# Attention with residual on one core: ScalarE empties the shared PSUM bank, the value bias moves to the residual, and the softmax sums take a way through DRAM

## The chip, the core and the metric

The kernel runs on one core of a Trainium2 chip. The core has five engines that each work through a queue of their own in order: TensorE (PE, matrix products, into the accumulation memory PSUM), VectorE (DVE), ScalarE (ACT), GpSimd (POOL) and SyncE (SP), which here only issues DMA transfers. The metric is device time in microseconds (us). The kernel before took 2355.27 us (median of 3 runs, 2353.17 to 2355.44).

## The reference

The input is x, 32 images of 256 channels on 32 x 32 places, in 32 bits throughout. Each image is normalised by groups of 8 channels, projected to queries, keys and values, goes through causal attention with 8 heads of 32 channels over its 1024 places, and is added to x:

```python
x = x + _L0_conv_ref(_gn(x), q_w, q_b, kv_w, kv_b)
# in _L0_conv_ref:
mask = jnp.tril(jnp.ones((S, S)), -1)                 # strictly before: place 0 sees nothing
scores = jnp.einsum('bhqd,bhkd->bhqk', q, k) / sqrt(dk)
scores = jnp.where(mask == 0, -10000.0, scores)
attn = jnp.where(mask == 0, 0.0, softmax(scores))
out = jnp.einsum('bhqk,bhkd->bhqd', attn, v)
```

For every place but the first the weights of a row add up to 1, so a bias on the values may as well be added to the result. Place 0 gets nothing, and its output is x alone.

## The kernel before

The work of one image is cut into 20 steps, written `(g, hf, k)`: g is one of two groups of four heads, hf one of two halves of 512 queries, k a block of 128 keys; half 0 has 3 steps, half 1 has 7. Steps are numbered 0 to 19 within an image below: 3 to 9 are group 0, half 1, and 13 to 19 group 1, half 1. A step's `scores` is four concurrent products of 512 queries into two pairs of PSUM banks (tile sT), an exponential of each pair on ACT (tile e), and on the diagonal a select on POOL that zeroes what a query must not see. Two steps later (LAG) `values` multiplies e with the values (tile acc), and DVE adds e onto a running sum of the group's first e tile. Behind the last step of a (g, hf), ACT copies acc to num, and one step later `sums` multiplies the running sum by ones (tile pd), so that the sums over all keys come out of PE. There are four such sums per image, in the steps 5, 12, 15 and, for the last, step 2 of the next image.

Between these, PE does the projections of the next image: eight units for queries and keys (tile pp) and four for the values (ppv), and two small products for the group averages of the image after next (pm and pv). All of pp, ppv, pm, pv and pd use one single PSUM bank (`misc`, pool ps_m with one buffer): each product must wait until the one before it has been read out. ACT reads pp, DVE reads ppv, pm, pv and pd.

The order is written by hand. `when(i, f)` puts f into step i, behind that step's scores and before its values, and `after` puts it behind the values. Each engine's queue is the order in which this loop emits its instructions:

```python
scores(*steps[i])
for f in at.get(i, ()): f()
values(*steps[i - LAG])
for f in after.get(i, ()): f()
```

An image's results are finished in the next image: DVE checks that the sums lie in a sane range, takes their reciprocals in four pieces of 128 columns, SP spreads these over 32 partitions per head (tile rb), DVE multiplies num by rb, POOL adds x and overwrites place 0, and SP writes the result.

## Time and profile before

| | |
|---|---|
| median of 3 runs | 2355.27 us |
| the profiled execution | 2354.04 us |
| its span in the trace | 2352.0 us, granted TensorE clock 0.951 |
| PE busy | 2113.2 us (90%) |
| DVE busy | 1732.8 us (74%) |
| ACT busy | 1358.9 us (58%) |
| POOL busy | 722.1 us (31%) |

The trace names an instruction by its line and tiles, "v<-ppv,v_bias" for a read of ppv and v_bias that writes v. A timeline row has the start, the duration, the engine and line, and in brackets how long the engine stood idle before it and what ended that. A row of the list of waits has the waiting engine and line, what it waited for, and then the total, the number of times and the longest. A row of the windows has for each engine its busy time, and behind POOL's the clock that TensorE was granted, 1.00 being the full one.

### The profile page before, as it was taken

The page shows a single profiled execution, that of the slowest core. Times are in us where ns is not written, and L with a number is a line of the kernel's source. Part 1 is how long each engine was busy: PE and PEld are TensorE (multiplying, and loading weights), DVE is VectorE, ACT ScalarE, POOL GpSimd, SP SyncE. Part 2 cuts the span into 40 slices and gives each one's busy share as a digit, 9 for nine tenths or more (in the row PEclk, how much of TensorE's full clock was granted, in tenths as well). Part 3 has the DMA queues.
Part 4 walks back from the last instruction along what each step waited for, and adds up shares of the span by engine and source line. Part 5 has one row for each costly group of instructions (what it writes and reads, how often), then busy time and mean ns, then how long its engine had stood idle before and what let it go on. Part 6 is the DMA issues. An engine that isn't in the chain of part 4 may idle for free.

```text
span 2352.0 us, 49835 instructions
## 1 busy us (share of the span) xinstructions
PE 2113.2 (90%) x22030; PEld 748.7 (32%) x22030; DVE 1732.8 (74%) x1641; ACT 1358.9 (58%) x1665; POOL 722.1 (31%) x689
## 2 busy tenths in 40 slices
PE   4999998899998999988999989899889999898995
PEld 1333333333333333333333333333333323333331
DVE  2577678777777777787777787777877777877787
ACT  1656655556555566555566555665555655556663
POOL 0232233322332322333223323223332233232245
PEclk9999999999999999999999999999999999999997
DMA  2001111011111010111011110111110111101001
GB/s 88 2 28 46 37 55 55 36 38 48 44 55 55 28 46 37 55 55 43 30 54 38 55 55 28 46 37 55 55 54 20 55 37 55 55 28 46 19 37 73
DMA packets 38078, 104.84 MB, mean 45 GB/s; under 512 B 4192, under 2 KB 5088, under 8 KB 37856
## 3 DMA queue, kind: packets, MB, share of 16 engines
q1 hardware_dynamic: 37856, 101.60, 11.8%
q8 instruction: 174, 2.85, 0.5%
q14 instruction: 48, 0.39, 0.1%
HBM read 34.47 MB, written 33.55 MB: 29 GB/s over the span
## 4 chain that ended last, share of the span: by engine, by line
PE 54%; DVE 40%; issue 5%; ACT 1%; DMA 0%; POOL 0%; SPq 0%; DVEq 0%; POOLq 0%; ACTq 0%
DVE e L270 24%; PE pp L130 16%; PE sT L234 12%; PE acc L265 11%; PE ppv L130 10%; PE pd L282 4%; DVE st L144 3%; DVE rec L301 2%; DVE den L290 2%; DVE rb L319 2%; DVE dev L156 1%; DVE xn L172 1%; DVE in_range L295 1%; DVE in_range L294 1%; DVE dev L157 1%
## 5 line engine op out<-in xcount | busy, mean ns | idle before, releaser
L241 ACT ACTIVATE e<-sT 128x1024 f32<-128x1024 f32 (+1 forms) x1280 | 1126.0, 939 | 629.4 <-PE sT L234 532.5
L270 DVE TENSOR_TENSOR e<-e,e 128x2048 f32<-128x2048 f32 (+3 forms) x640 | 1162.7, 1817 | 84.9 <-POOL e L247 48.7
L247 POOL TENSOR_SCALAR_AFFINE_SELECT e<-e 128x512 f32<-128x512 f32 (+1 forms) x384 | 443.3, 1162 | 1464.1 <-ACT e L241 1464.0
L234 PE MATMUL sT<-q,k 32*128 32x512 f32 (+3 forms) x6144 | 710.1, 525 | 0.5 <-ACT e L241 0.5
L265 PE MATMUL acc<-e,v 128*32 128x512 f32 (+3 forms) x6144 | 623.1, 493 | 6.7 <-POOL e L247 4.2
L130 PE MATMUL pp<-xn,wT 128*32 128x512 f32 x4096 | 494.2, 600 | 13.9 <-DVE den L288 7.8
L130 PE MATMUL ppv<-wT,xn 128*32 128x256 f32 x4096 | 297.1, 439 | 154.2 <-DVE rstd L164 143.7
L234 PEld LDWEIGHTS sT<-q,k 32*128 32x128 f32 x6144 | 299.1, 183 | 420.6 <-issue 283.2
L265 PEld LDWEIGHTS acc<-e,v 128*32 128x32 f32 x6144 | 176.4, 112 | 391.4 <-issue 309.2
L290 DVE TENSOR_TENSOR den<-den,pd 128x512 f32<-128x512 f32 x96 | 66.0, 687 | 285.0 <-PE pd L282 285.0
L320 POOL TENSOR_TENSOR rb<-rb,x 128x512 f32<-128x512 f32 x128 | 226.0, 1766 | 131.3 <-DVE rb L319 95.7
L204 DVE TENSOR_TENSOR v<-ppv,v_bias 128x512 f32<-128x512 f32 x128 | 88.0, 687 | 211.5 <-PE ppv L130 211.5
L130 PEld LDWEIGHTS ppv<-wT,xn 128*32 128x32 f32 x4096 | 132.9, 123 | 296.4 <-DVE rstd L164 146.3
L130 PEld LDWEIGHTS pp<-xn,wT 128*32 128x32 f32 x4096 | 107.0, 109 | 318.7 <-issue 201.8
L274 ACT COPY num<-acc 128x512 f32<-128x512 f32 x128 | 74.3, 580 | 224.7 <-PE acc L265 224.7
L282 PE MATMUL pd<-e,pick 128*32 128x512 f32 x1024 | 137.3, 608 | 23.4 <-DVE e L270 23.2
L189 ACT ACTIVATE q<-pp,qk_bias 128x512 f32<-128x512 f32 x128 | 88.2, 689 | 68.8 <-PE pp L130 63.6
L301 DVE RECIPROCAL rec<-den 128x128 f32<-128x128 f32 x128 | 120.2, 941 | 0.0
L189 ACT ACTIVATE k<-pp,qk_bias 128x512 f32<-128x512 f32 x128 | 88.2, 689 | 41.0 <-PE pp L130 39.3
L319 DVE TENSOR_TENSOR rb<-num,rb 128x512 f32<-128x512 f32 x128 | 91.8, 718 | 2.4 <-DMA rb<-rec 2.4
L144 DVE BATCH_NORM_STATS2 st<-x 128x6 f32<-128x512 f32 x128 | 80.1, 668 | 4.6 <-DMA x<-in_x_dram 4.6
L282 PEld LDWEIGHTS pd<-e,pick 128*32 128x32 f32 x1024 | 23.9, 108 | 125.7 <-DVE e L270 60.2
(40 smaller groups left out, 280.9 us busy)
## 6 DMA issues: line engine op xcount, KB each, us to landing
x<-in_x_dram SPq DMA_DIRECT2D x32, 1024.0 KB, 5.8
rb<-rec SPq DMA_DIRECT2D x128, 256.0 KB, 2.5
out_dram<-rb SPq DMA_DIRECT2D x64, 512.0 KB, 3.0
wn<-in_L_conv_kv_w_dram SPq DMA_DIRECT2D x2, 256.0 KB, 3.3
wn<-in_L_conv_q_w_dram SPq DMA_DIRECT2D x1, 256.0 KB, 2.8
v_bias<-in_L_conv_kv_b_dram SPq DMA_DIRECT2D x1, 128.0 KB, 3.0
qk_bias<-in_L_conv_q_b_dram SPq DMA_DIRECT2D x1, 1.0 KB, 3.3
qk_bias<-in_L_conv_kv_b_dram SPq DMA_DIRECT2D x1, 1.0 KB, 3.0
```

The lines of the kernel that those rows point to most:

```text
L130: nc.tensor.matmul(out[part], lhsT=lhsT[:, part], rhs=rhs, start=start, stop=stop, skip_group_check=True)
L144: nc.vector.bn_stats(st[:, c, :], live["x", b][:, g, c * HALF : (c + 1) * HALF])
L189: nc.scalar.activation(live[key][:, cols], pp, AF.Identity, bias=qk_bias[:, n, g : g + 1], scale=(SCALE, 1.0)[n],)
L234: nc.tensor.matmul(pairs[j // 2][:, j % 2, cols], lhsT=kk[rows, kb * P : (kb + 1) * P], rhs=q[rows, hf * HALF + of.start : hf * HALF + of. ...
L241: nc.scalar.activation(e[:, 2 * a : 2 * a + 2, c0:], pairs[a][:, :, c0:], AF.Exp)
L247: nc.gpsimd.affine_select(out=diagonal, in_=diagonal, pattern=[[0, 4], [0, n], [1, P]], compare_op=ALU.is_gt, fill=0.0, base=0, channel_mu ...
L265: nc.tensor.matmul(acc[HD * j : HD * (j + 1), of], lhsT=live["v", b][:, kb, h * HD : (h + 1) * HD], rhs=e[:, j, cols], start=k == 0, stop= ...
L270: nc.vector.tensor_add(total[:, :, of], total[:, :, of], e[:, :, cols])
L282: nc.tensor.matmul(pd[HD * j : HD * (j + 1), :], lhsT=pick[:, n, :], rhs=total[:, j, :], start=True, stop=True, skip_group_check=True,)
L301: nc.vector.reciprocal(live["rec", b][:, cols], live["den", b][:, cols])
L319: nc.vector.tensor_mul(rb[:, g, cols], num[:, g, cols], rb[:, g, cols])
L320: nc.gpsimd.tensor_add(rb[:, g, cols], rb[:, g, cols], xt[:, g, cols])
```

## The change

Four things change together.

- ACT instead of DVE reads the shared bank everywhere: the mean, the variance (with 1e-5 added as a bias), the values and the sums.
- The values carry no bias any more. DVE's last step adds the bias of the channel and x in one instruction (line 327 of the new file), and the corner copy goes to DVE too; POOL has no part in the finish.
- The sums of the four (g, hf) are each copied to SBUF by ACT and written to DRAM by SP. When all are there, `gather` reads them back as 128 rows of 64 values, DVE checks and inverts these, SP writes the inverses to DRAM, and the spread reads them from there.
- The steps to which things are given: the load two steps earlier, the pieces of the preparation to steps 4, 5, 8, 10, 16, 18 in place of 3, 5, 8, 11, 14, 16, the projections so that no two products on the shared bank stand in one step, check and inversion at step 5 of the next image, and the finish at 11, 12, 14, 15 of the next image in place of 11 to 14 behind an end that was counted one step later.

```diff
-    pick = const.tile([P, 4, HD], F32, name="pick")
...
+    pick = const.tile([P, HD], F32, name="pick")
+    nc.gpsimd.memset(pick, 1.0)
...
+        dram = tc.alloc_tile_pool(name="dram", bufs=2, space=bass.MemoryType.DRAM)
...
-            nc.vector.tensor_copy(mean, pm[:, :NG])
+            nc.scalar.copy(mean, pm[:, :NG])
...
-            nc.vector.tensor_scalar_add(rstd, pv[:, :NG], 1e-5)
+            nc.scalar.activation(rstd, pv[:, :NG], AF.Identity, bias=eps)
...
-            nc.vector.tensor_add(
-                live["v", b][:, 2 * n : 2 * n + 2, :], pp, v_bias.unsqueeze(1).broadcast_to([P, 2, C])
-            )
+            nc.scalar.copy(live["v", b][:, 2 * n : 2 * n + 2, :], pp)
...
-                    pd[HD * j : HD * (j + 1), :], lhsT=pick[:, n, :], rhs=total[:, j, :],
+                    pd[HD * j : HD * (j + 1), :], lhsT=pick, rhs=total[:, j, :],
...
+            den = small.tile([P, HALF], F32, tag="den", name=f"den_{b}_{n}")
+            nc.scalar.copy(den, pd)
             if n == 0:
-                live["den", b] = small.tile([P, HALF], F32, tag="den", name=f"den_{b}")
-                nc.vector.tensor_copy(live["den", b], pd)
-            else:
-                nc.vector.tensor_add(live["den", b], live["den", b], pd)
...
+                live["sums", b] = dram.tile([4, 4, HALF], F32, tag="sums", name=f"sums_{b}")
+            nc.sync.dma_start(out=live["sums", b][n], in_=den[::HD, :])
+
+        def spread_rows(t):
+            return t.rearrange("n j (r c) -> (n j r) c", c=ROW)
+
+        def gather(b):
+            live["rows", b] = small.tile([P, ROW], F32, tag="rows", name=f"rows_{b}")
+            nc.sync.dma_start(out=live["rows", b], in_=spread_rows(live["sums", b]))
+
+        def invert(b):
+            rows = live["rows", b]
+            nc.vector.scalar_tensor_tensor(in_range, rows, SUM_MIN, in_range, ALU.is_ge, ALU.mult)
+            nc.vector.scalar_tensor_tensor(in_range, rows, SUM_MAX, in_range, ALU.is_le, ALU.mult)
+            inv = small.tile([P, ROW], F32, tag="inv", name=f"inv_{b}")
+            nc.vector.reciprocal(inv, rows)
+            live["inv", b] = dram.tile([4, 4, HALF], F32, tag="inv", name=f"inverses_{b}")
+            nc.sync.dma_start(out=spread_rows(live["inv", b]), in_=inv)
...
-                    in_=rec[n::4, :].unsqueeze(1).broadcast_to([P // 4, 4, HALF]),
+                    in_=live["inv", b][n].unsqueeze(1).broadcast_to([4, HD, HALF]),
...
-            nc.gpsimd.tensor_add(rb[:, g, cols], rb[:, g, cols], xt[:, g, cols])
+            nc.vector.scalar_tensor_tensor(
+                rb[:, g, cols], rb[:, g, cols], v_bias_col[:, g : g + 1], xt[:, g, cols], ALU.add, ALU.add
+            )
             if hf == 0:
-                nc.gpsimd.tensor_copy(rb[:, g, 0:1], xt[:, g, 0:1])
+                nc.vector.tensor_copy(rb[:, g, 0:1], xt[:, g, 0:1])
...
-                when(b * N, lambda b=b: load(b + 2))
-                for n, f in zip((3, 5, 8, 11, 14, 16), prepare(b + 2)):
+                when(max(b * N - 2, 0), lambda b=b: load(b + 2))
+                for n, f in zip((4, 5, 8, 10, 16, 18), prepare(b + 2)):
                     when(b * N + n, f)
...
-                    when(b * N + 1 + n * N // len(units), f)
+                for n, f in zip((1, 3, 4, 6, 7, 9, 11, 13, 14, 16, 17, 19), projections(b + 1)):
+                    when(b * N + n, f)
...
-            end = (b + 1) * N + LAG + 2
-            when(end, lambda b=b: check_sums(b))
-            for c in range(BPH):
-                when(end + 1 + c, lambda b=b, c=c: invert(b, c))
-            when(end + BPH, lambda b=b: spread(b))
-            for n in range(4):
-                when(end + BPH + 3 + n, lambda b=b, n=n: finish(b, n))
+            end = (b + 1) * N + LAG + 1
+            when(end, lambda b=b: gather(b))
+            when(end + 2, lambda b=b: invert(b))
+            when(end + 2, lambda b=b: spread(b))
+            for n, at_step in enumerate((8, 9, 11, 12)):
+                when(end + at_step, lambda b=b, n=n: finish(b, n))
```

What this does to the queues is shown at two places. The first is DVE around steps 8 to 11 of image 4, before. The names carry image, group, half and key block; `dev_6` belongs to the preparation of image 6, `v_5` to the projection of image 5, `rb_3` to the finish of image 3, and the e tiles to image 4 itself.

```order
L155 TENSOR_TENSOR dev_6_2875<-mv_6_2717,mean_6_2873 128x2
L156 TENSOR_TENSOR dev_6_2875<-dev_6_2875 128x2
L157 TENSOR_TENSOR dev_6_2875<-dev_6_2875,mv_6_2717 128x2
L270 TENSOR_TENSOR e0_4_0_1_0_2708<-e0_4_0_1_0_2708,e_4_0_1_3_2788 128x2048
L204 TENSOR_TENSOR v_5_2824<-ppv_5_1_2894,v_bias_122 128x512
L270 TENSOR_TENSOR e0_4_0_1_0_2708<-e0_4_0_1_0_2708,e_4_0_1_4_2813 128x2048
L270 TENSOR_TENSOR e0_4_0_1_0_2708<-e0_4_0_1_0_2708,e_4_0_1_5_2848 128x4x384
L270 TENSOR_TENSOR e0_4_0_1_0_2708<-e0_4_0_1_0_2708,e_4_0_1_5_2848 128x4x128
L319 TENSOR_TENSOR rb_3_2863<-num_3_2185,rb_3_2863 128x512
L164 TENSOR_SCALAR rstd_6_2960<-pv_6_2955 128x2
```

The same place in the changed kernel, up to the addition that the second sum (pd) needs:

```order
L159 TENSOR_TENSOR dev_6_2915<-mv_6_2775,mean_6_2913 128x2
L160 TENSOR_TENSOR dev_6_2915<-dev_6_2915 128x2
L161 TENSOR_TENSOR dev_6_2915<-dev_6_2915,mv_6_2775 128x2
L273 TENSOR_TENSOR e0_4_0_1_0_2735<-e0_4_0_1_0_2735,e_4_0_1_3_2836 128x2048
L273 TENSOR_TENSOR e0_4_0_1_0_2735<-e0_4_0_1_0_2735,e_4_0_1_4_2860 128x2048
L273 TENSOR_TENSOR e0_4_0_1_0_2735<-e0_4_0_1_0_2735,e_4_0_1_5_2894 128x4x384
L273 TENSOR_TENSOR e0_4_0_1_0_2735<-e0_4_0_1_0_2735,e_4_0_1_5_2894 128x4x128
L326 TENSOR_TENSOR rb_3_2813<-num_3_2213,rb_3_2813 128x512
L327 SCALAR_TENSOR_TENSOR rb_3_2813<-rb_3_2813,v_bias_col_120,x_3_879 128x512
L331 COPY rb_3_2813<-x_3_879 128x1
L273 TENSOR_TENSOR e0_4_0_1_0_2735<-e0_4_0_1_0_2735,e_4_0_1_6_2924 128x4x256
```

The v addition and the read of pv have left DVE's queue, and the whole first quarter of the finish stands ahead of the last addition.

The second place is ACT in steps 8 to 11 of the same image, in the changed kernel, where these reads now stand.

```order
L244 ACTIVATE e_4_0_1_5_2894<-sT_4_0_1_5_0_2895 128x1024
L244 ACTIVATE e_4_0_1_5_2894<-sT_4_0_1_5_1_2896 128x1024
L156 COPY mean_6_2913<-pm_6_2908 128x2
L244 ACTIVATE e_4_0_1_6_2924<-sT_4_0_1_6_0_2925 128x2x256
L244 ACTIVATE e_4_0_1_6_2924<-sT_4_0_1_6_1_2926 128x2x256
L209 COPY v_5_2870<-ppv_5_1_2934 128x512
L244 ACTIVATE e0_4_1_0_0_2957<-sT_4_1_0_0_0_2958 128x1024
L244 ACTIVATE e0_4_1_0_0_2957<-sT_4_1_0_0_1_2959 128x1024
L168 ACTIVATE rstd_6_2973<-pv_6_2968,eps_75 128x2
L244 ACTIVATE e_4_1_0_1_2986<-sT_4_1_0_1_0_2987 128x1024
L244 ACTIVATE e_4_1_0_1_2986<-sT_4_1_0_1_1_2988 128x1024
L209 COPY v_5_2870<-ppv_5_2_3003 128x512
```

Each read stands behind the two exponentials of its own step. On PE, pv moves one step forward, from the step of a projection of values to a step without one, and the fourth such projection moves from step 12 to step 13.

More of the change, by code (lines that the diff above doesn't have):

```diff
@@ L26 @@
 SUM_MAX = 1.0e20
+ROW = 64
 LAG = 2
@@ L71, in tile_norm_attention_residual @@
     nc.gpsimd.memset(power, -0.5)
-    pick = const.tile([P, 4, HD], F32, name="pick")
-    nc.gpsimd.memset(pick, 0.0)
-    for n in range(4):
-        nc.gpsimd.memset(pick[:, n, n::4], 1.0)
+    pick = const.tile([P, HD], F32, name="pick")
+    nc.gpsimd.memset(pick, 1.0)
     avg = const.tile([P, P // CPG, CPG], F32, name="avg")
@@ L88, in tile_norm_attention_residual @@
     avg = avg.rearrange("p a b -> p (a b)")
-    in_range = const.tile([P, HALF], F32, name="in_range")
+    in_range = const.tile([P, ROW], F32, name="in_range")
     nc.gpsimd.memset(in_range, 1.0)
+    eps = const.tile([P, 1], F32, name="eps")
+    nc.gpsimd.memset(eps, 1e-5)
     wT = const.tile([P, NG, 3 * C], F32, name="wT")
@@ L106, in tile_norm_attention_residual @@
     nc.vector.tensor_scalar_mul(qk_bias[:, 0, :], qk_bias[:, 0, :], SCALE)
+    v_bias_col = const.tile([P, NG], F32, name="v_bias_col")
+    nc.sync.dma_start(out=v_bias_col, in_=kv_b[C : 2 * C].rearrange("(g p) -> p g", p=P))
     v_bias = const.tile([P, C], F32, name="v_bias")
@@ L118, in unshifted @@
         ps_m = tc.alloc_tile_pool(name="ps_m", bufs=1, space=PSUM)
-        pools = [xpool, work, qkpool, epool, small, ps_s, ps_o, ps_m]
+        pools = [xpool, work, qkpool, epool, small, dram, ps_s, ps_o, ps_m]
         live = {}
@@ L352, in unshifted @@
                     when(b * N + s + LAG + 1, lambda b=b, g=g, hf=hf: sums(b, g, hf), after)
-            end = (b + 1) * N + LAG + 2
-            when(end, lambda b=b: check_sums(b))
-            for c in range(BPH):
-                when(end + 1 + c, lambda b=b, c=c: invert(b, c))
-            when(end + BPH, lambda b=b: spread(b))
-            for n in range(4):
-                when(end + BPH + 3 + n, lambda b=b, n=n: finish(b, n))
+            end = (b + 1) * N + LAG + 1
[4 more added lines that the diff above has]
+                when(end + at_step, lambda b=b, n=n: finish(b, n))
         with tc.manual_schedule(engines={ENG.PE, ENG.Activation, ENG.DVE, ENG.Pool}):
```

12 lines of the change are left out of this document (removed).

## Prediction

> **What bounds the kernel now.** I read the page first, then the list of waits, then the timeline of one image, then the granted clock in small windows.
>
> ```profile
> span 2352.0 us, 49835 instructions
> PE 2113.2 (90%) x22030; PEld 748.7 (32%) x22030; DVE 1732.8 (74%) x1641; ACT 1358.9 (58%) x1665; POOL 722.1 (31%) x689
> ...
> PE ppv L130 <- DVE rstd L164: 143.7, 30, 4.9
> ...
> PE pd L282 <- DVE e L270: 23.2, 31, 2.6
> ...
> PE pp L130 <- DVE den L288: 7.8, 29, 0.3
> ```
>
> TensorE (PE) is 90% busy and every other engine has room, so PE's program order is the clock of the loop. It loses time in one place: 30 times a value projection (ppv) waits until VectorE (DVE) has read pv out of the one shared bank, 143.7 us in all, which is 29 times the 4.87 us seen below and a short one. Images 1 to 29 have it: image 0 has no image before it to finish, and 30 and 31 have none to prepare. Everything else PE waits for is small. The timeline shows why DVE is late; the rows run from step 8 of an image to its second sum, and the last one is step 8 of the next image.
>
> ```profile
> 1011.86 1.15 PE L234 MATMUL sT<-q,k 32*128 32x384 f32 x16
> ...
> 1013.04 2.92 ACT L241 ACTIVATE e<-sT 128x1024 f32<-128x1024 f32 x4 [1.86 <-PE sT L234]
> ...
> 1015.00 0.16 DVE L155 TENSOR_TENSOR dev<-mv,mean 128x2 f32<-128x2 f32 x1
> ...
> 1015.05 1.73 POOL L247 TENSOR_SCALAR_AFFINE_SELECT e<-e 128x1024 f32<-128x1024 f32 x2 [3.12 <-ACT e L241]
> ...
> 1016.72 2.28 DVE L270 TENSOR_TENSOR e<-e,e 128x2048 f32<-128x2048 f32 x1
> ...
> 1018.92 0.68 DVE L204 TENSOR_TENSOR v<-ppv,v_bias 128x512 f32<-128x512 f32 x1
> ...
> 1019.52 5.93 DVE L270 TENSOR_TENSOR e<-e,e 128x2048 f32<-128x2048 f32 x3
> ...
> 1021.05 0.24 PE L130 MATMUL pv<-dev,avg 128*32 128x2 f32 x8
> ...
> 1025.37 0.68 DVE L319 TENSOR_TENSOR rb<-num,rb 128x512 f32<-128x512 f32 x1
> 1025.97 0.14 DVE L164 TENSOR_SCALAR rstd<-pv 128x2 f32<-128x2 f32 x1
> ...
> 1026.17 3.64 PE L130 MATMUL ppv<-wT,xn 128*32 128x256 f32 x32 [4.87 <-DVE rstd L164]
> ...
> 1030.86 1.93 PE L130 MATMUL ppv<-wT,xn 128*32 128x256 f32 x32
> ...
> 1032.12 0.73 POOL L247 TENSOR_SCALAR_AFFINE_SELECT e<-e 128x512 f32<-128x512 f32 x1 [3.81 <-ACT e L241]
> ...
> 1033.60 1.07 PE L282 MATMUL pd<-e,pick 128*32 128x512 f32 x8
> ...
> 1083.54 1.15 PE L234 MATMUL sT<-q,k 32*128 32x384 f32 x16
> ```
>
> pv is finished at 1021.3, but its reader L164 stands in DVE's queue behind three sum additions and a finishing multiplication, and runs at 1025.97. The restart is dear too: the ppv at 1026.17 takes 3.64 us where the next takes 1.93, 1.71 more. The clock rows of this image and the next say why.
>
> ```profile
> 1022.50:1023.00 0.50, 0.00 (x0) 0.00 (x0) 0.50 (x1) 0.43 (x1) 0.00 (x1) 0.93 0.00 0
> 1029.50:1030.00 0.50, 0.50 (x12) 0.20 (x4) 0.12 (x1) 0.00 (x0) 0.00 (x0) 0.74 0.00 0
> 1094.18:1094.68 0.50, 0.00 (x0) 0.00 (x0) 0.50 (x1) 0.43 (x1) 0.00 (x1) 0.93 0.00 0
> 1101.18:1101.68 0.50, 0.50 (x12) 0.20 (x4) 0.12 (x1) 0.00 (x0) 0.00 (x0) 0.74 0.00 0
> ```
>
> The seventh number is the granted clock. It is half from about 1022.85 (a window's mean of 0.93) to about 1029.7 (0.74), some 6.83 us, and the same stretch returns exactly 71.68 us later, which is also the step from 1011.86 to 1083.54. 71.68 is 21 times 3.413, half of the stretch. I read this as a grid of 3.41 us on which the clock falls and recovers: PE resumes, runs at half clock up to the next line of the grid, and by this the image's period settles on whole cells, 21 of them. Without the slow restart it would be about 70.0.
>
> **The change, part by part.** *The stall at ppv goes.* ScalarE (ACT) now reads pv directly behind the two exponentials of its own step, about 3.2 us after that step's scores start, and PE wants the bank 3.3 us after. I cost this wait at 0.1 us. If ACT were a step late it would be 3 us, but ACT keeps up: its work in a step with a projection is two exponentials (1.9 us) and one copy against PE's 3.8.
>
> *What is late next* is the sum of the second group. Its matmul (pd) at step 12 needs the last addition of step 11, and DVE's new order before that is: dev chain, additions of steps 8 to 10, then the whole finish of the first quarter (multiply, add, corner copy), then that addition. The dev chain cannot start before ACT has copied the mean, and ACT does so after both exponentials of step 8; everything behind it on DVE is held as well. From the rows, with time zero at 1011.86:
>
> - dev starts at 3.14 now. The select on e at 1015.05 (3.19) shows when the exponentials are done; I add a copy of 0.2 us and take 3.35.
> - From there to the end of the three additions now takes 1025.45 − 1015.00 = 10.45, less the v addition, which leaves DVE (1019.52 − 1018.92 = 0.60): 9.85, which contains the selects of GpSimd (POOL) that share this stretch. End at 13.2.
> - Multiply 0.68, the new add 0.69, corner copy 0.1, and 0.1 for waiting on each other's output: 1.55. Then the addition of 1024 columns, 1.22. That is 16.0.
> - The select that today falls after the stall (1032.12, 0.73) now falls into this stretch: 16.7.
>
> PE could be there earlier. Its unit costs are steps between starts where nothing waits:
>
> ```profile
> 1062.19 0.61 PE L265 MATMUL acc<-e,v 128*32 128x256 f32 x8
> ...
> 1062.74 0.71 PE L234 MATMUL sT<-q,k 32*128 32x256 f32 x8
> ...
> 1063.38 1.92 PE L130 MATMUL pp<-xn,wT 128*32 128x512 f32 x16
> ...
> 1067.11 1.14 PE L234 MATMUL sT<-q,k 32*128 32x512 f32 x8
> ...
> 1080.82 1.93 PE L130 MATMUL ppv<-wT,xn 128*32 128x256 f32 x32
> ...
> 1082.57 1.04 PE L265 MATMUL acc<-e,v 128*32 128x512 f32 x8
> ```
>
> A short acc is 0.55, short scores 0.64, a projection 1.75, a full acc 0.97 (to 1083.54). With pv done at 9.4 that gives ppv, short acc, short scores, full acc: 13.3, and 0.1 for the restart, 13.4. **So PE waits 3.3 us at pd instead of 4.9 us at ppv.** The second sum starts at 16.7; today it starts at 1033.60 − 1011.86 = 21.74 with one more projection ahead of it (1.75, moved to step 13).
>
> The rest of the image, from that sum to the next step 8, takes 1083.54 − 1033.60 = 49.94. It gets the moved projection, +1.75, and loses the small waits of the list above, 0.75 at pd and 0.27 at pp: 50.7. Natural period 16.7 + 50.7 = 67.4 against about 70.0.
>
> *The clock.* A 3.3 us gap in PE is more than twice the 1.5 us (1021.3 to 1022.85) after which the clock fell here, so I expect half clock again. Bounds: no loss at all, or 1.71 as now. On the grid the next whole number of cells above 67.4 is 20, 68.27, a loss of 0.9 and inside the bounds, so I take 68.27: **3.41 us less per image.**
>
> The Trainium skill, in "TensorE: Matmul & The Clock Gate", section "What's actually happening", says that the clock is gated after at least one idle window of about 3.4 us, and that these windows run freely. The grid agrees; the fall after 1.5 us of idleness does not need a wholly idle window, and the rows decide.
>
> *Costs beside the path.*
>
> ```profile
> L274 ACT COPY num<-acc 128x512 f32<-128x512 f32 x128 | 74.3, 580 | 224.7 <-PE acc L265 224.7
> ...
> L288 DVE COPY den<-pd 128x512 f32<-128x512 f32 x32 | 20.5, 642 | 6.5 <-PE pd L282 6.5
> ...
> L294 DVE SCALAR_TENSOR_TENSOR in_range<-den,in_range 128x512 f32<-128x512 f32 x32 | 21.9, 683 | 0.0
> ...
> L301 DVE RECIPROCAL rec<-den 128x128 f32<-128x128 f32 x128 | 120.2, 941 | 0.0
> ...
> rb<-rec SPq DMA_DIRECT2D x128, 256.0 KB, 2.5
> ...
> qk_bias<-in_L_conv_kv_b_dram SPq DMA_DIRECT2D x1, 1.0 KB, 3.0
> ```
>
> ACT gains eight copies of 0.58 and two tiny reads per image, some 5 us on 42; it has 25 us of room, and PE's 3.8 us steps cover each copy. The Trainium skill, in "ScalarE: Activation LUTs", section "Rules for kernel authors", speaks against this: adds and the like belong on VectorE, up to three times faster. At three times 0.642 the eight copies would be 15 us per image, and where an exponential pair, a v copy and a num copy meet in one step (1.94 + 1.93 + 0.58 against PE's 3.4 us in step 11) PE would wait 1 us, 29 us in all. The rows contradict it for reads from PSUM in 32 bits: 580 ns on ACT, 642 on DVE.
>
> DVE loses four reciprocals (3.76), four bias additions (2.75), four den operations (2.7) and most of two checks (1.4); it gains four adds of the row L294's kind (2.75) and a reciprocal of 64 columns (0.47 by half of L301). Net about −7 us per image, but only what stands between steps 8 and 12 counts, and that is in the sum. POOL's residual adds go.
>
> The DRAM legs: den copy 0.6 after the fourth sum, then a write and a gather. Small transfers of before land in 3.0 us, so the row of sums is back 6.8 us after the fourth sum. DVE reaches its check at about 4.2 and stops there for some 2.6 us, with the statistics of the second half and two additions behind it (7.1 us of work with the check). These must be done by the mean, 17.7 + 3.35 = 21 us after the sum (step 3 starts right behind the fourth sum, in the trace at 1067.11, so 16.4 to the next step 8, plus one projection, less 0.5 of waits), so the gather may land as late as 13.9. Cover: 7 us. The inverses go out and come back in two more legs (3.0 and 2.5), near 14; the multiplication that reads them stands near 30. SP issues 13 transfers per image in place of 7, each under 0.6 us, in 68 us. All this costs nothing inside the loop.
>
> *Edges.*
>
> ```profile
> 2243.78 1.93 PE L130 MATMUL ppv<-wT,xn 128*32 128x256 f32 x32 [1.76 <-DVE v L204]
> ...
> 2303.66 1.93 PE L282 MATMUL pd<-e,pick 128*32 128x512 f32 x8 [1.96 <-DVE e L270]
> ...
> 2332.59 0.69 DVE L290 TENSOR_TENSOR den<-den,pd 128x512 f32<-128x512 f32 x1 [2.06 <-PE pd L282]
> ...
> 2338.05 2.49 SPq L309 DMA_DIRECT2D rb<-rec  x4
> ```
>
> From the last den operation to the issue of the spread it now takes 5.5 us, with nothing beside it; with a copy, three legs and a short check it will be 0.6 + 9.0 + 0.9 = 10.5, so +5, less up to 3 because POOL no longer follows with the last additions. The last two images may lose the waits of 1.76 and 1.96 in the rows, and a half clock, 0 to −5. I take zero for both together, between −5 and +5.
>
> Sum: 2354.04 (the profiled execution) − 29 × 3.41 = 2255.2; the median of the runs shown stands 1.2 above that execution, so **2256 us**.
>
> **Rivals.**
>
> 1. *The gap does not lower the clock.* The period is then the natural 67.4: 29 × 4.3 = 124 us, 2231. For it: the gap is 1.6 us shorter than now, and the page on the clock gate asks for a whole idle window, which 3.3 us is not. Against: half clock began 1.5 us into the gap. 0.12.
> 2. *DVE is not late at pd.* If selects and dev chain cost 2 us less than in today's rows, PE's wait falls under 1.5 us and the clock stays: period 13.4 + 50.7 = 64.1 up to 65.5, saving 29 × 6.2 to 7.6, 2135 to 2176. For it: POOL's residual adds no longer compete with DVE. Against: none of them stood in the stretch that I took over. 0.15.
> 3. *The gather comes late* (slower). DVE waits at its check for the row of sums in front of all additions. It decides once a leg takes over 6.6 us (13.9 = 0.6 + 2 legs); at 10 us a leg the gather lands at 20.6, the image grows by 6.7 to 74.1, 22 cells, 75.1: 29 × 3.4 more, 2454. Against: the transfers quoted above landed in 2.5 and 3.0 us. 0.06.
> 4. *The change moves the stall without gain.* If the finish on DVE holds pd 3 us longer than I sum (stt slower, more selects in between), the period falls back to 21 cells: 2355. 0.05; something between that and my forecast, 2290 to 2345: 0.10.
>
> My forecast itself, 2235 to 2290: 0.52.
>
> **Numbers.** The range 2150 to 2290 takes in the forecast, the first rival and half of the second, about 0.75 to 0.8. A difference under 0.2% (about what a measurement of this kernel can tell from none) has 0.04; slower 0.07, from the third rival and the tail of the fourth; faster 0.89.
>
> **What would show it.** Right: no wait of ppv on pv's reader; a wait of about 3 us per image of pd on DVE's additions; half clock still once per image, 68.3 us apart; ACT near 1510 us busy, DVE near 1510, POOL near 470. Wrong: pd without a wait and no half clock (second rival), DVE idle at its check for over 10 us (third), ppv waiting for ACT, or a period of 71.7.

## The result, and the profile after

The changed kernel takes 2264.35 us (median of 4 runs, 2263.33 to 2264.6) where the kernel before took 2354.82 beside it: a ratio of 0.9616, with a 95% interval of 0.9599 to 0.9633. The profiled execution took 2263.33 us, with a span of 2261.6. All lines from here on are numbered as in the file they come from; in the changed kernel L156 reads the mean, L168 pv, L209 the values and L291 the sums (all on ACT), L273 adds up e, L326 and L327 are the finish on DVE, L305 the check, L316 the spread.

The first part of the changed kernel's page:

```profile
span 2261.6 us, 50192 instructions
...
PE 2081.9 (92%) x22030; PEld 733.3 (32%) x22030; DVE 1514.2 (67%) x1417; ACT 1492.0 (66%) x1985; POOL 419.3 (19%) x494
```

The list of waits of the changed kernel:

```profile
DVE dev L159 <- ACT mean L156: 203.0, 32, 6.7
...
PE pd L286 <- DVE e L273: 92.2, 32, 3.4
...
PE ppv L134 <- ACT mean L156: 8.0, 30, 0.3
```

The wait of 143.7 us of ppv on pv's reader is gone, and PE now waits 92.2 us for DVE's additions at pd. The timeline of one image, from step 8 to the second sum (the idle time ahead of a row is in brackets):

```profile
972.15 1.15 PE L237 MATMUL sT<-q,k 32*128 32x384 f32 x16
...
975.35 1.09 DVE L159 TENSOR_TENSOR dev<-mv,mean 128x2 f32<-128x2 f32 x1 [6.74 <-ACT mean L156]
...
977.19 7.55 DVE L273 TENSOR_TENSOR e<-e,e 128x2048 f32<-128x2048 f32 x4
...
981.42 1.93 PE L134 MATMUL ppv<-wT,xn 128*32 128x256 f32 x32
...
984.53 2.26 POOL L250 TENSOR_SCALAR_AFFINE_SELECT e<-e 128x1024 f32<-128x1024 f32 x2
...
984.66 1.59 DVE L326 TENSOR_TENSOR rb<-num,rb 128x512 f32<-128x512 f32 x1
986.28 1.04 DVE L327 SCALAR_TENSOR_TENSOR rb<-rb,v_bias_col,x 128x512 f32<-128x512 f32 x1
...
987.43 1.22 DVE L273 TENSOR_TENSOR e<-e,e 128x1024 f32<-128x1024 f32 x1
...
988.70 1.94 PE L286 MATMUL pd<-e,pick 128*32 128x512 f32 x8 [3.00 <-DVE e L273]
```

ACT reads pv in time, and the ppv at 981.42 starts without a wait and takes 1.93 us, where before one took 3.64. DVE stands idle for 6.74 us until ACT has copied the mean, then works without a pause, and the second sum begins 16.55 us after step 8's scores, 3.00 us after PE could have begun it. Its 1.94 us are nearly twice the 1.07 of an undisturbed one. The windows of this image show why (the seventh number is the granted clock):

```profile
988.00:989.00 1.00, 0.30 (x4) 0.20 (x8) 1.00 (x2) 0.00 (x0) 0.00 (x0) 0.87 0.00 0
989.00:990.00 1.00, 1.00 (x8) 0.00 (x0) 0.96 (x3) 0.00 (x0) 0.00 (x0) 0.50 0.00 0
...
992.00:993.00 1.00, 1.00 (x16) 0.42 (x16) 1.00 (x2) 0.49 (x1) 0.00 (x0) 0.92 0.21 78
```

The clock falls at 988.74 (0.87 is a quarter of a microsecond at half) and is back at 992.16: half clock for 3.42 us, once per image, where it was 6.83.

**Where the 90.4 us of span went.** The product pm of the image after next stands once in every image. Between the fourth and the last of them lie 28 images. The windows from the one to the other, before and after (busy time of PE, its weight load, DVE, ACT and POOL, then the mean clock):

```profile
151.50:2159.80 2008.30, 1841.02 (x19268) 653.68 (x19264) 1513.40 (x1429) 1188.20 (x1456) 616.70 (x588) 0.95 0.13 45
```

```profile
150.10:2072.10 1922.00, 1815.85 (x19271) 639.44 (x19267) 1322.35 (x1232) 1303.53 (x1736) 359.50 (x420) 0.97 0.14 49
```

28 images take 2008.3 and 1922.0 us, 71.73 and 68.64 each: 86.3 of the 90.4 are here. PE's idle time fell from 167.3 to 106.2 (61.1 less), its busy time by 25.2. Ahead of the loop lie 1.4 us, behind it 2.7.

### The profile page after: what moved, and what is told of

Its sections match the earlier page's. It is cut to its first block, busy times and chain, and to the rows that moved or that the text cites. A ratio compares the mean times of both kernels' runs of the same rounds, so it can differ in the third digit from the quotient of the medians.

```text
span 2261.6 us, 50192 instructions
## 1 busy us (share of the span) xinstructions
PE 2081.9 (92%) x22030; PEld 733.3 (32%) x22030; DVE 1514.2 (67%) x1417; ACT 1492.0 (66%) x1985; POOL 419.3 (19%) x494
## 4 chain that ended last, share of the span: by engine, by line
PE 73%; DVE 19%; ACT 4%; issue 3%; DMA 1%; POOL 1%; SPq 0%; DVEq 0%; POOLq 0%; ACTq 0%
PE sT L237 23%; PE pp L134 21%; PE acc L268 17%; DVE e L273 12%; PE ppv L134 6%; PE pd L286 6%; DVE rb L326 2%; ACT e L244 2%; DVE dev L159 1%; DVE rb L327 1%; DVE dev L160 1%; ACT num L277 1%; ACT q L193 1%; POOL e L250 1%; DMA rb<-inverses 0%
## 5 line engine op out<-in xcount | busy, mean ns | idle before, releaser
L273 DVE TENSOR_TENSOR e<-e,e 128x2048 f32<-128x2048 f32 (+3 forms) x640 | 1088.6, 1701 | 492.1 <-PE acc L268 192.0
L237 PE MATMUL sT<-q,k 32*128 32x512 f32 (+3 forms) x6144 | 721.2, 541 | 0.5 <-ACT e L244 0.5
L250 POOL TENSOR_SCALAR_AFFINE_SELECT e<-e 128x512 f32<-128x512 f32 (+1 forms) x384 | 351.0, 926 | 1781.9 <-ACT e L244 1042.2
L134 PE MATMUL ppv<-wT,xn 128*32 128x256 f32 x4096 | 257.9, 394 | 10.9 <-ACT mean L156 8.0
L286 PE MATMUL pd<-e,pick 128*32 128x512 f32 x1024 | 150.1, 657 | 92.2 <-DVE e L273 92.2
L291 ACT COPY den<-pd 128x512 f32<-128x512 f32 x128 | 75.2, 588 | 184.4 <-PE pd L286 184.4
L159 DVE TENSOR_TENSOR dev<-mv,mean 128x2 f32<-128x2 f32 x32 | 33.1, 1035 | 203.0 <-ACT mean L156 203.0
L326 DVE TENSOR_TENSOR rb<-num,rb 128x512 f32<-128x512 f32 x128 | 114.6, 896 | 9.8 <-DMA rb<-inverses 9.8
L209 ACT COPY v<-ppv 128x512 f32<-128x512 f32 x128 | 75.1, 587 | 51.2 <-PE ppv L134 50.7
L327 DVE SCALAR_TENSOR_TENSOR rb<-rb,v_bias_col,x 128x512 f32<-128x512 f32 x128 | 105.4, 824 | 4.6
```

Source lines behind the costliest of these rows:

```text
L134: nc.tensor.matmul(out[part], lhsT=lhsT[:, part], rhs=rhs, start=start, stop=stop, skip_group_check=True)
L237: nc.tensor.matmul(pairs[j // 2][:, j % 2, cols], lhsT=kk[rows, kb * P : (kb + 1) * P], rhs=q[rows, hf * HALF + of.start : hf * HALF + of. ...
L250: nc.gpsimd.affine_select(out=diagonal, in_=diagonal, pattern=[[0, 4], [0, n], [1, P]], compare_op=ALU.is_gt, fill=0.0, base=0, channel_mu ...
L273: nc.vector.tensor_add(total[:, :, of], total[:, :, of], e[:, :, cols])
L286: nc.tensor.matmul(pd[HD * j : HD * (j + 1), :], lhsT=pick, rhs=total[:, j, :], start=True, stop=True, skip_group_check=True,)
L326: nc.vector.tensor_mul(rb[:, g, cols], num[:, g, cols], rb[:, g, cols])
```

## The experiments

My theory: DVE's chain mean, dev, additions, finish, last addition sets the second sum; the gap that PE has there lowers its clock; and the way through DRAM costs nothing in the loop. The rivals: that something else holds pd (the new order of the projections, ACT, the DRAM legs), that the clock loss has another cause, or that the gain comes from the new step table and not from the engines.

### What holds the second sum

`e_finish_late` takes the first quarter's finish out of the chain by giving the finish two steps later.

```diff
-            for n, at_step in enumerate((8, 9, 11, 12)):
+            for n, at_step in enumerate((10, 11, 13, 14)):
```

> The changed kernel with the four finishing pieces two steps later (13, 14, 16, 17), so that none of them stands in front of the addition that the second sum (pd) needs. Chain theory: in the trace of the changed kernel the first piece takes 984.66 to 987.43, 2.8 us, of a chain that makes PE wait 3.0 us at pd; the wait falls to about 0.3 us, the half clock goes with it (1.7 us), the period goes from 68.6 to about 64.3, and the time to about 2140 us. Rival (the wait at pd is not set by DVE's queue, or moves to the next sum): 2230 to 2264 us, with the half clock still there.

Measured: 2162.24 us, ratio 0.9173 (0.9147 to 0.92). The timeline at the second sums of two images in a row, and DVE's additions ahead of the later one:

```profile
882.46 1.07 PE L286 MATMUL pd<-e,pick 128*32 128x512 f32 x8 [1.13 <-DVE e L273]
...
937.86 9.58 DVE L273 TENSOR_TENSOR e<-e,e 128x2048 f32<-128x2048 f32 x5
...
947.50 1.06 PE L286 MATMUL pd<-e,pick 128*32 128x512 f32 x8 [1.13 <-DVE e L273]
```

The finish was on the path: the wait falls from 3.00 to 1.13, the clock stays up (0.992 in the mean of the run, 0.970 in the changed kernel), and an image takes 65.04 us. It came slower than expected, because these 1.13 us of wait stayed: the finish took 2.77 us of the chain (984.66 to 987.43 above), but the five additions, the last of which now runs beside POOL's selects, take 9.58 us where they took 7.55 and 1.22.

`e_mean_after` shortens the chain at its other end: the mean is worked out behind step 8's values, so that DVE does one addition while it would have waited for the mean.

```diff
-                    when(b * N + n, f)
+                    when(b * N + n, f, after if n == 8 else at)
```

> The changed kernel with the mean of step 8 given behind the values of that step instead of ahead of them: the dev chain, which waits for ACT's copy of the mean, then stands behind one addition of 2048 columns (2.3 us) that it blocks now. Chain theory: the second sum starts 2.3 us earlier, PE's wait falls from 3.0 to 0.7 us, too short for the half clock, period about 64.7, time about 2150 us. Rival (the finish in front of the last addition is what counts, and blocking is covered): less than 20 us faster, 2245 to 2264 us.

Measured: 2134.06 us, ratio 0.9054 (0.9027 to 0.908). From the timeline of one image:

```profile
920.65 1.09 DVE L159 TENSOR_TENSOR dev<-mv,mean 128x2 f32<-128x2 f32 x1 [4.35 <-ACT mean L156]
...
922.49 5.31 DVE L273 TENSOR_TENSOR e<-e,e 128x2048 f32<-128x2048 f32 x3
...
931.28 1.07 PE L286 MATMUL pd<-e,pick 128*32 128x512 f32 x8 [0.28 <-DVE e L273]
```

DVE's idle time before dev is 4.35 instead of 6.74, three additions stand behind dev instead of four, and pd waits 0.28, less than the 0.7 expected.

`e_both_late` makes both moves.

> Both moves at once, the finish two steps later and the mean behind the values. Chain theory: no wait at pd at all, no half clock, PE's own work sets the period: 13.4 + 50.3 = 63.7 us, 29 x 4.9 less than 2264, about 2122 us. Rival (something else on PE's way becomes the bound near 66 us): about 2190 us.

Measured: 2118.8 us, ratio 0.8989 (0.8963 to 0.9015), the fastest version that does the whole work, level with `e_no_dram` below. The engines on its page:

```profile
PE 2027.0 (96%) x22030; PEld 736.6 (35%) x22030; DVE 1518.0 (72%) x1417; ACT 1491.6 (70%) x1985; POOL 410.6 (19%) x494
```

And in its list of waits:

```profile
PE pd L286 <- DVE e L273: 2.8, 1, 2.8
```

DVE and ACT are as busy as after the change, and PE waits for DVE at pd once, in the last image. Two lines of the step table, with no work removed, are worth another 145 us.

`e_no_select` leaves POOL's selects out (and with them the mask on the diagonal), to see what they cost DVE.

```diff
-            if d >= 0:
+            if d > 99:
```

> The changed kernel without POOL's selects (places after a query are not masked, so the result is another one). Contention theory: DVE's instructions with two inputs in SBUF and POOL's selects block each other whole; without them the dev chain takes 0.6 in place of 1.8 us, the additions 6.9 in place of 7.5, the first finishing piece 1.6 in place of 2.8; the second sum starts 3 us earlier, PE does not wait, no half clock: about 2125 us. Rival (the selects only fill DVE's idle time): within 20 us of 2264 us.

Measured: 2118.8 us, ratio 0.8987 (0.8957 to 0.9018). The group of DVE's finishing multiplications (busy time, mean ns of one, idle time ahead), first after the change, then without selects:

```profile
L326 DVE TENSOR_TENSOR rb<-num,rb 128x512 f32<-128x512 f32 x128 | 114.6, 896 | 9.8 <-DMA rb<-inverses 9.8
```

```profile
L326 DVE TENSOR_TENSOR rb<-num,rb 128x512 f32<-128x512 f32 x128 | 87.6, 684 | 9.8 <-DMA rb<-inverses 9.8
```

One multiplication took 896 ns in the mean and takes 684 without selects; the one at 984.66 above took 1.59 us beside the select at 984.53. The first subtraction for dev, 1.09 us at 975.35 above, is among the shortened ones:

```profile
916.17 0.16 DVE L159 TENSOR_TENSOR dev<-mv,mean 128x2 f32<-128x2 f32 x1 [6.75 <-ACT mean L156]
```

In the image that this row is from, dev takes 0.47 us instead of 1.84, the four additions 7.13 instead of 7.55, and the finish 1.58 instead of 2.77: together the 3.0 us that PE waited. With DVE and POOL out of each other's way the chain is short enough, and the image takes 63.83 us. The Trainium skill says in "SBUF — State Buffer", section "Who interferes with whom", that a DVE instruction with two inputs in SBUF contends with a GpSimd instruction that reads SBUF; these rows agree. So the wait shrinks or ends when the finish, the mean, both, or the selects beside them are taken out of this one chain; the chain is shown.

### The clock by itself

`e_warm_pd` leaves the chain and the wait, and gives PE 12 products to do meanwhile, whose results are overwritten.

```diff
+            for j in range(12 if n == 1 else 0):
+                nc.tensor.matmul(
+                    pd[HD * (j % 4) : HD * (j % 4 + 1), :], lhsT=pick, rhs=wT[:, 0, 0:HALF],
+                    start=True, stop=True, skip_group_check=True,
+                )
```

> The changed kernel with 12 useless products of 512 columns ahead of the second sum of each image, into the same bank, that wait for nothing: PE has some 2.6 us of work while it now waits 3.0 us. The sum itself cannot start earlier. Grid theory of the clock: without the gap the clock stays full, the 1.5 to 1.7 us of slow running per image go, 2264 less 29 x 1.6 gives about 2217 us. Rival (the slow products behind the wait are a cost of restarting and not of the clock): 2264 us or more.

Measured: 2219.1 us, ratio 0.9415 (0.9387 to 0.9442). The timeline at one image's second sum (L291 here, behind the added products):

```profile
899.64 2.78 PE L286 MATMUL pd<-wT,pick 128*32 128x512 f32 x24
902.86 0.64 PE L291 MATMUL pd<-e,pick 128*32 128x512 f32 x4 [0.43 <-DVE e L273]
```

The sum comes no sooner (16.56 us after step 8's scores, 16.55 before), but PE's work behind it runs at full clock (0.993 in the mean of the run), and an image takes 66.92 us instead of 68.64: 45 us in all come from the clock alone, 1.6 to 1.7 per image. 66.92 is the natural period of the changed kernel.

### Which part of the change brings what

`e_order_only` gives the kernel before the new steps for preparation and projections, and nothing else.

```diff
-                for n, f in zip((3, 5, 8, 11, 14, 16), prepare(b + 2)):
+                for n, f in zip((4, 5, 8, 10, 16, 18), prepare(b + 2)):
...
-                units = projections(b + 1)
-                for n, f in enumerate(units):
-                    when(b * N + 1 + n * N // len(units), f)
+                for n, f in zip((1, 3, 4, 6, 7, 9, 11, 13, 14, 16, 17, 19), projections(b + 1)):
+                    when(b * N + n, f)
```

> The kernel before with nothing but the new steps for the preparation (4, 5, 8, 10, 16, 18) and the projections; every read stays on DVE, the sums stay in SBUF. Order theory: the read of pv then stands one step earlier in DVE's queue, at about 10.2 us behind the start of step 8, and PE wants the bank for the next ppv at 9.4, so that wait falls from 4.9 to about 0.9 us; the second sum comes at about 16.5 as in the changed kernel; 2250 to 2275 us, so that the order alone gives nearly the whole gain. Engine theory (ACT's reading of the bank is what helps): the wait at ppv stays 3 us or more, 2320 us or more.

Measured: 2274.59 us, ratio 0.9648 (0.9613 to 0.9684). The opposite, `e_old_order`, is the changed kernel with the old steps for these (the same lines the other way round):

> The changed kernel with the old steps for the preparation (3, 5, 8, 11, 14, 16) and the projections, so pv and a ppv stand in one step again, now read by ACT. Both theories have PE wait about 2.1 us at that ppv for ACT's exponentials of step 11. Order theory: the wait at pd shrinks by as much, since DVE's chain is unchanged, half clock stays: 2225 to 2270 us. Engine theory the same or less. If the new order were needed for the gain, 2330 us or more.

Measured: 2203.03 us, ratio 0.9345 (0.9312 to 0.9377), faster than I expected (pd no longer waits, and the half clock comes in about every second image) and 61 us faster than the whole change. `e_norm_on_act` is the kernel before with the mean and pv read by ACT:

```diff
-            nc.vector.tensor_copy(mean, pm[:, :NG])
+            nc.scalar.copy(mean, pm[:, :NG])
...
-            nc.vector.tensor_scalar_add(rstd, pv[:, :NG], 1e-5)
+            nc.scalar.activation(rstd, pv[:, :NG], AF.Identity, bias=eps)
```

> The kernel before with only the mean and pv read by ACT; order, values, sums and finish as before. Engine theory: the wait at ppv falls from 4.9 to about 2.1 us (ACT's exponentials of step 11), the second sum comes near 18 us behind step 8, where DVE still has the values to read, half clock stays: 2260 to 2285 us. If reading the values and the sums on ACT, too, is needed: 2320 us or more.

Measured: 2256.23 us, ratio 0.957 (0.9537 to 0.9603), just under the range expected. PE's waits in the three, in this order:

```profile
PE pd L282 <- DVE e L270: 81.3, 33, 3.0
```

```profile
PE ppv L134 <- ACT rstd L168: 56.5, 30, 1.9
...
PE pd L286 <- DVE e L273: 3.7, 2, 2.8
```

```profile
PE ppv L132 <- ACT rstd L166: 56.5, 30, 1.9
```

So the parts don't add up. The order alone brings about 81 us, two tiny reads on ACT alone about 99, and all of the change 90; the values and sums on ACT, the value bias, the finish on DVE and the earlier load weren't tried alone. With the old order the old stall at ppv shrinks to 1.9 us, because ACT reads pv behind one step's exponentials, and this wait together with the projection that still stands ahead of pd gives DVE the time that it needs there. The new order takes both away, PE comes to pd 3 us early, and the wait is longer than the one that it replaced. These two runs also show what a wait of 1.9 us does to the clock; the windows of `e_old_order` are from two neighbouring images, in which PE waits from 826.0 and from 893.3:

```profile
829.00:830.00 1.00, 1.00 (x16) 0.51 (x12) 1.00 (x2) 0.00 (x0) 1.00 (x2) 0.52 0.00 0
...
896.00:897.00 1.00, 1.00 (x24) 0.63 (x20) 1.00 (x1) 0.00 (x0) 1.00 (x2) 1.00 0.00 0
```

The same gap lowers the clock in one image (0.52 at 829, 1.2 us after PE's restart) and not in the next (1.00 at 896); images of 67.3 to 67.4 and of 65.7 us alternate, with few exceptions.

`e_steps_only` asks whether the best step table needs the moved reads at all: the kernel before with the new steps, the mean behind the values of step 8, and the finish later.

> The kernel before with new steps alone: those of the changed kernel for preparation and projections, the mean behind the values, the finish at 13, 14, 16, 17. No instruction changes its engine. Order theory: DVE reaches the last addition before the second sum about 14 us behind the start of step 8, PE wants it near 14, no half clock, period 64.5 to 66 us: 2140 to 2190 us. Rival (with 54 us of work per image DVE cannot keep up, and the moves to ACT are needed): 2220 us or more.

Measured: 2252.27 us, ratio 0.9566 (0.9547 to 0.9586), a miss for the theory that the order would be enough. One image's timeline:

```profile
906.34 2.22 DVE L270 TENSOR_TENSOR e<-e,e 128x2048 f32<-128x2048 f32 x1
...
908.68 3.53 PE L130 MATMUL ppv<-wT,xn 128*32 128x256 f32 x32 [2.37 <-DVE mean L152]
```

On DVE the mean's read now stands behind an addition, and holds the shared bank for 2.37 us; half clock follows in every image, 3.53 us for the projection. On ACT (`e_mean_after`) the same move cost nothing. So this step table needs the other engines: under it, the moves between engines are worth about 131 us (2252.27 to the 2120.78 of `e_no_dram` below, which has them all but the way through DRAM, and also has the earlier load). A table that suits the reads on DVE wasn't sought.

### The way through DRAM

`e_no_dram` is `e_both_late` with sums, check, reciprocals and spread as before, on DVE and from SBUF.

> The kernel with both late moves, and the way through DRAM undone: DVE reads the sums out of the bank, checks and inverts 128 x 512 of them as the kernel before does, and the spread reads SBUF; all else as in the changed kernel. In the loop DVE has 7 us more per image in 64 us, with 7 us of slack ahead of the mean; PE's next product waits some 0.3 us for DVE's read as before: 0 to +10 us over 32 images. Behind the last image, where the changed kernel takes 28 us from the last sum to the end and the kernel before 19.4 us, the difference comes back, less the bias step on DVE: -8 us. Theory that DRAM only costs the tail: 2105 to 2120 us against 2118.8. Rival (the way through DRAM keeps DVE free in the loop, and without it PE waits a microsecond per sum): 2150 us or more.

Measured: 2120.78 us, ratio 0.9011 (0.8996 to 0.9026): 0.8 us above the range expected and the same as `e_both_late`, though DVE has more to do (1726.6 us busy, 1518.0 with the way through DRAM). The image takes 63.72 us here and 63.70 there. In the last image the two differ and cancel. Its fourth sum and the first use of the spread, first without DRAM, then `e_both_late`:

```profile
2093.84 1.93 PE L287 MATMUL pd<-e,pick 128*32 128x512 f32 x8 [4.98 <-DVE e L275]
...
2103.68 0.69 DVE L324 TENSOR_TENSOR rb<-num,rb 128x512 f32<-128x512 f32 x1 [2.40 <-DMA rb<-rec]
```

```profile
2087.26 1.93 PE L286 MATMUL pd<-e,pick 128*32 128x512 f32 x8 [2.75 <-DVE e L273]
...
2100.52 0.69 DVE L326 TENSOR_TENSOR rb<-num,rb 128x512 f32<-128x512 f32 x1 [6.29 <-DMA rb<-inverses]
```

Without DRAM the last sum is 6.6 us later, and the end comes 6.7 us sooner after it: spans of 2116.9 and 2117.0. So once both moves are made, the way through DRAM neither costs nor brings anything in the loop. Whether it brings something in the changed kernel itself, where DVE's chain holds PE up, wasn't tried.

`e_trips2` and `e_trips6` send the row of sums two and six more times through SBUF and DRAM, 4 and 12 legs, before the check reads it.

```diff
         def gather(b):
+            for r in range(2):
+                there = small.tile([P, ROW], F32, tag="there", name=f"there_{b}_{r}")
+                nc.sync.dma_start(out=there, in_=spread_rows(live["sums", b]))
+                live["sums", b] = dram.tile([4, 4, HALF], F32, tag=f"trip{r}", name=f"trip_{b}_{r}")
+                nc.sync.dma_start(out=spread_rows(live["sums", b]), in_=there)
```

> The changed kernel with the sums taken through SBUF and DRAM two more times ahead of the gather, four more legs. Legs measure 1.8 us each in the changed kernel's tail, so the gather lands 7.3 us later, at about 11.7 us behind the last sum, before the 13.9 us that I worked out as the latest: nothing in the loop, +7 us behind the last image, 2272 us. If the cover is smaller than 7 us, every microsecond beyond it costs 29 to 31 us.

> The same with six more trips, twelve legs, 22 us: the gather lands at about 26 us behind the last sum, 12 us later than 13.9, with DVE standing at its check in front of all additions. The third rival's mechanism: 12 us per image and 22 at the end, 2600 to 2680 us. If DVE's stop is covered elsewhere: under 2400 us.

Measured: 2277.95 us, ratio 0.9675 (0.9656 to 0.9695), and 2558.69, ratio 1.0868 (1.0842 to 1.0894). With four more legs the loop keeps its period (68.62 us in the mean, 68.64 in the changed kernel) and its wait at pd (3.0), though DVE stands 6 to 8 us at its check in each image (11.8 behind the last); the 13.6 us are paid at the two ends of the program, some 6.4 of them at the last check. With twelve the third rival comes about, at 8.3 us per image and not the 12 expected. From the list of waits of `e_trips6`:

```profile
PE pm L134 <- DVE mv L149: 243.6, 31, 9.3
```

And the timeline of one image:

```profile
976.50 1.07 PE L286 MATMUL pd<-e,pick 128*32 128x512 f32 x8
...
1001.79 0.23 DVE L310 SCALAR_TENSOR_TENSOR in_range<-rows,in_range 128x64 f32<-128x64 f32 x1 [19.70 <-DMA rows<-trip]
...
1004.27 0.29 PE L134 MATMUL pm<-mv,avg 128*32 128x2 f32 x8 [7.98 <-DVE mv L149]
```

The fourth sum is the row at 976.50; the check gets its row of sums 25.3 us later and PE then waits 7.98 us. By these rows one that came 17.3 us after the sum would not have held PE up; in the last image of the changed kernel it came after 5.4.

## Why the prediction held, point by point

The forecast was 2256 us, measured were 2264.35: the likeliest case, inside its range. That it came so close is in part luck: two terms were mis-sized, and their errors have opposite signs.

- *The stall at ppv goes, and ACT is not late:* right. The wait on pv's reader is gone; 8.0 us of waits on the copied mean remain, 0.27 per image. The copies on ACT cost 587 and 588 ns each, close to the 580 taken. The factor of three that the prediction set against ACT is given in the Trainium skill, in "ScalarE: Activation LUTs", section "Rules for kernel authors", for bf16; this kernel works in 32 bits throughout, so the rows are another case and don't contradict it.
- *What is late next:* right, with errors of up to 0.6 us in its links that nearly cancel. Predicted and measured in the image shown: dev starts at 3.35 and 3.20 us, the additions end at 13.2 and 12.6, the finish takes 1.55 and, with two selects beside it, 2.77 (I had put 0.73 for a select behind it), the second sum starts at 16.7 and 16.55, PE's wait is 3.3 and 3.00. The experiments on the chain confirm it.
- *The clock:* right in kind. Half clock comes once per image and `e_warm_pd` prices it. I took 0.9 us of loss on a natural period of 67.4; they are 1.6 to 1.7 on 66.92. Both terms were mis-sized, with opposite signs. In the kernel before, the prediction read the window's 0.93 as a fall at 1022.85 and counted 1.5 us of idleness ahead of it; 0.93 puts it at 1022.93, which makes it 1.6.
- *A lock on 20 cells, 68.27 us:* wrong. The images took 68.3 to 68.55 us, and the half clock came a little earlier in each, until it covered two cells in one image and began again: three times in the profile, in images of 69.9 to 70.2 us. The mean of all is 68.64. 28 times 0.37 is 10 us, which is more than the whole miss. What stopped the lock is in the rows of two neighbouring images, the first with its second sum at 507.89, the next at 576.21:

```profile
507.00:508.00 1.00, 0.10 (x4) 0.11 (x8) 1.00 (x2) 0.00 (x0) 0.00 (x0) 0.73 0.00 0
...
510.00:511.00 1.00, 1.00 (x8) 0.28 (x8) 0.97 (x2) 0.48 (x1) 0.00 (x0) 0.56 0.95 381
...
575.00:576.00 1.00, 0.00 (x0) 0.00 (x0) 1.00 (x2) 0.00 (x0) 0.00 (x0) 0.87 0.00 0
...
582.00:583.00 1.00, 1.00 (x20) 0.44 (x13) 1.00 (x2) 0.14 (x1) 0.00 (x0) 0.72 0.00 0
```

  In the first the clock falls at 507.46, 0.43 us before PE resumes, and is back at 510.88. In the next it falls at 575.74, 0.47 before, and is back only at 582.56. The sooner the clock falls before PE resumes, the less busy time runs at half and the shorter the image, but at 0.47 the cell no longer counts as busy. In the whole loop the clock came back after cells with up to 0.45 us of idleness, and stayed low after the three with more. A period of 68.27 would have needed a fall beyond that edge. `e_steps_only`, whose images took 68.26 us in the mean and hardly drift, shows that such a lock exists where the natural period lies right.
- *DRAM legs free in the loop:* right, and with more cover than I gave them: a leg took 1.8 us and not 3.0, and by the rows of `e_trips6` the row of sums could come 17.3 us after the fourth sum, not 13.9. The stop of 2.6 us per image at the check didn't come: DVE waited there 9.2 us in the whole run, 5.4 of them behind the last image.
- *Edges at zero:* nearly. From the start of the last sum to the end of the span it was 21.4 us before and is 29.0, so +7.6 where I had put +2 to +5; the images ahead of it made up for it (2.7 us gained behind the loop). The tail of the changed kernel:

```profile
2232.59 1.06 PE L286 MATMUL pd<-e,pick 128*32 128x512 f32 x8 [2.79 <-DVE e L273]
...
2234.34 0.48 SPq L294 DMA_DIRECT2D sums<-den  x1
2236.13 0.33 SPq L301 DMA_DIRECT2D rows<-sums  x1
2237.97 0.22 DVE L305 SCALAR_TENSOR_TENSOR in_range<-rows,in_range 128x64 f32<-128x64 f32 x1 [5.43 <-DMA rows<-sums]
...
2240.41 2.46 SPq L316 DMA_DIRECT2D rb<-inverses  x4
2245.20 0.69 DVE L326 TENSOR_TENSOR rb<-num,rb 128x512 f32<-128x512 f32 x1 [6.29 <-DMA rb<-inverses]
...
2247.87 0.69 DVE L326 TENSOR_TENSOR rb<-num,rb 128x512 f32<-128x512 f32 x1 [1.00 <-DMA rb<-inverses]
```

  The legs were cheaper than I had put, but the spread from DRAM was dearer: 4.79 us from its issue to the first multiplication, against 2.39 before (2338.05 to 2340.44, from SBUF), and DVE then waits 1.0 to 1.3 us for each further quarter, where before the four came without a wait between them:

```profile
2340.44 3.63 DVE L319 TENSOR_TENSOR rb<-num,rb 128x512 f32<-128x512 f32 x4 [2.42 <-DMA rb<-rec]
```

- *Busy times:* ACT 1510 predicted and 1492.0, DVE 1510 and 1514.2, POOL 470 and 419.3.
- *The rivals:* no half clock (2231) is not what happened, but its time is about that of `e_warm_pd`. DVE not late at pd (2135 to 2176) is what two moved lines bring about, at 2118.8. The late gather came only with twelve more legs, at 77 us per image; the prediction's 75.1 was for a gather of 20.6 us, the run's came after 25.3.
- *The chances:* the parts of the range that the prediction names add up to 0.715 (0.52, 0.12 and half of 0.15), not to 0.75 to 0.8.

Not settled: PE's idle time fell by 61.1 us over 28 images and its busy time by 25.2, 0.9 per image. At half clock PE does about as much as before (3.7 us per image, 3.65 now), so the clock is not the reason. With the part at half clock counted by half, PE's busy time per image is 63.9 us before and 63.0 now; it is 64.0 in `e_norm_on_act`, which keeps the old steps, and 63.1 in `e_order_only`, which has the new ones and nothing else. So the 0.9 goes with the new steps; which products overlap better in them isn't taken apart.

## What to carry to other kernels

When a stall is removed, work out when the next product in the same queue will be ready, and which engine's chain makes it so: here the wait came back, 3 us instead of 5, at the next product that needs VectorE, and two moved lines in the step table then were worth more than the whole rewrite. A gap of 2.4 to 3 us in TensorE was paid twice here, as the gap and as a stretch of half clock behind it, and one of 1.1 us only once, so the shorter one is worth far less effort; useless products in a gap can be cheaper than idleness. Do the parts of a change also by themselves: here two tiny reads alone did as well as the whole (2256 and 2264 us), and the whole without its new steps beat it (2203).

## What the chip showed that I had not expected

- *When the clock falls and returns.* In these runs a gap of 1.13 us never lowered the clock, one of 1.89 did in about half of the images, and gaps of 2.37 to 3.0 did in every image. The clock changes only on a grid of 3.41 us (the falls at 575.74 and 988.74 above are 121 cells apart), so the place of a gap on the grid counts beside its length. 1.78 us of work in a cell did not keep the clock up in the kernel before (1019.52 to 1022.93, idle from 1021.3), while some 0.47 us of idleness in a cell was enough to keep it down. How much of the gap lies in one cell doesn't settle it alone: in `e_old_order` PE works 1.52 us in the cell from 1156.72 and 1.53 in the one from 1224.98, and the clock falls behind the first and not behind the second. What decides between them is open. The Trainium skill has in "TensorE: Matmul & The Clock Gate", section "What's actually happening", a free-running window of 3413 ns, which the grid confirms, and a throttle after at least one idle window; here much less than a wholly idle window was enough.
- *A period that nearly locks.* Where the loss depends on the phase of the grid, the image's time drifts (68.55 to 68.3 us in the changed kernel) and slips every seven to ten images; a median of several runs hides this, a list of the products' starts shows it.
- *The source of the spread matters.* Four transfers of 256 KB from DRAM reach their first reader 4.8 us after the issue, the same from SBUF after 2.4, while the small write and read of the sums took 1.8 us each from issue to what followed. The two spreads also differ in shape (each row of DRAM is read 32 times, each one of SBUF 4 times), so that DRAM alone is the cause isn't shown.
